# Own rows of layer 1: nine places in place of six

## The chip, the cores and the metric

The kernel runs on one core of one Trainium2 chip. The metric is the device time of one execution in microseconds. Four runs of the kernel before gave 989.70, 991.78, 993.73 and 992.79 us, with a median of 992.29 us.

## The reference, cut to what matters

The program is a stack of four graph layers over 2708 nodes with 512 features each. `adj` is a sparse matrix with a full diagonal, about five values in a row. Every layer ends in a residual sum and a layernorm. Layer 1, which the change is about, is this:

```python
type_sum_a = adj_a @ x
type_sum_b = adj_b @ x
attn_a = sigmoid(concatenate([type_sum_a, x], axis=1) @ Wa.T + ba)
attn_b = sigmoid(concatenate([type_sum_b, x], axis=1) @ Wb.T + bb)
h = x @ W_sa
s_left = h @ a_sa[0, :Hd]
s_right = h @ a_sa[0, Hd:]
scores = s_left[:, None] + s_right[None, :]
e = where(adj_a != 0, exp(-leaky_relu(scores, 0.01)), 0.0)
attn = e / (sum(e, axis=1, keepdims=True) + 1e-05)
x_a = attn @ h
x_b = adj_b @ (x @ W_gcnb) + b_gcnb
x = layernorm(x + sigmoid(attn_a * x_a + attn_b * x_b))
```

`adj_a` and `adj_b` are both `adj`. Layer 0 before it gives `layernorm(x + (x - (adj @ x) * (d + 1)) @ W + b)`. Layers 2 and 3 are sums over neighbours again, layer 3 with a last matmul and a tanh.

## The kernel before, in words

All is float32. The 2708 nodes are cut into 24 blocks of 113 rows (`R`, the last has 109), and for the dense products of layer 0 into 22 windows of 128 rows. Layer 0 finds the values of each block of `adj` off the diagonal and lists them in four chunks (`EC`) of 128 edges. From then on a sum over neighbours is, for each block, four indirect gathers of source rows (`gather`, L600, issued on the POOL queue) and matmuls of the gathered rows with a spread matrix of the edges' values. The diagonal is left out of the lists, so each block also needs its *own rows*, scaled by the diagonal.

For every window layer 0 computes `h` and `x @ W_gcnb` and stores both, with five more columns, as one row of 1029 floats (`W1`) in the DRAM table `table[0]` (`store0`, L1051). Layer 1 gathers whole rows from this table (`gather1`, L1371) into a ring of three buffers `gath`, and the own rows of block `i` are loaded from it by `load_own1(i)` (L634): 112 rows and 1 row of 1024 floats, two DMAs on the SP queue (`move_rows`, L564). They land in one of six places (`own_place`, L630): two in each of `shared[0]`, `shared[1]` and `w0_sb`, buffers that layer 0 uses for blocks of `adj` and for its weight.

The order is written out by hand: the instructions stand on every engine and queue as the program lists them. The places around the change are these:

- the end of layer 0 (loop at L1209 to L1283): blocks 0 to 3 are loaded in the step `k + 2 == NB` (L1263), blocks 4 and 5 in the step `k == NB` (L1280). After the loop come `keep_busy(4)`, eight matmul instructions that nobody reads, and the store of the last window, `store0(KB - 1)` (L1285);
- between the layers: `bg_bc` is loaded (L1499), small tables are made on DVE (L1308 to L1330), and `spread_left` (L1363) turns a column of `xr` into rows with PE transposes and DVE copies;
- layer 1's loop: step `i` issues `gather1(i + 2)`, then `sums1(i)` (PE, L1407), `both1(i - 1)` (DVE, with `l1a` at L1458), then `load_own1(i - 1 + NO)` into the place that `both1(i - 1)` has just read, then `scored_sums1(i)` (PE, L1417), `scores1(i + 1)` (DVE, `e` at L1390, the first that needs all of block `i + 1`'s gathers), `stats1(i - 1)`, `gates1(i)`, `gated1(i)` (DVE, `l1b` at L1437, the first reader of own rows), `mask1(i + 1)`, and `norm1(i - 1)`, which stores block `i - 1` of layer 1's result with two DMAs on the SP queue.

With `NO = 6` the loop loads blocks 6 to 23 in its steps 1 to 18; steps 19 to 23 load none.

Layer 0 also has these small rings from the pool `work`: two tiles `xi` (a block's own rows of `x`), two tiles `uT` (turned rows, also used by layer 3) and three tiles `uw` (turned windows).

Of the kernel before, what the change touches and what calls it, by code (L numbers as in the profile page):

```python
# [8 lines left out]
FP = mybir.dt.float32  # L9
# [3 lines left out]
P = 128  # L13
# [434 lines left out]
def sparse_stack(  # L448
# [30 lines left out]
    N, D = x.shape  # L479
# [4 lines left out]
    DB = D // P  # L484

    W1 = 2 * D + 5
# [4 lines left out]
    big = ctx.enter_context(tc.tile_pool(name="big", bufs=1))  # L491
    work = ctx.enter_context(tc.tile_pool(name="work", bufs=2))
    small = ctx.enter_context(tc.tile_pool(name="small", bufs=4))

    def rows(i):
        return min(R, N - i * R)
# [41 lines left out]
    def column(name, value):  # L538
        t = const.tile([P, NB], FP, name=name)
        nc.gpsimd.memset(t, value)  # L540
        return t
# [4 lines left out]
    adiag = column("adiag", 1.0)  # L546
# [17 lines left out]
    def move_rows(r, dst, src):  # L564

        c = r // 16 * 16
        for a, b in ((0, c), (c, r)):
            if a < b:
                nc.sync.dma_start(out=dst(a, b), in_=src(a, b))

    def turned(u, r, name):

        tr = ps_tr.tile([P, DB, P], FP, tag="tr", name=f"tr_{name}")
        for f in range(DB):
            nc.tensor.transpose(tr[:, f, :r], u[:r, f * P : (f + 1) * P], ident[:r, :r])
        uT = work.tile([P, DB, P], FP, tag="uT", name=f"uT_{name}")
        nc.scalar.copy(uT[:, :, :r], tr[:, :, :r])  # L577
        return uT

# [44 lines left out]

    shared = [big.tile([P, KB * R], FP, name=f"shared{k}") for k in range(2)]

    w0_sb = big.tile([P, DB, D], FP, name="w0_sb")
    NO = 6

    def own_place(i):  # L630
        t = (*shared, w0_sb.rearrange("p b d -> p (b d)"))[i % NO // 2]
        return t[:, i % 2 * 2 * D :][:, : 2 * D]

    def load_own1(i):  # L634
        r = rows(i)
        own1[i] = own_place(i)
        move_rows(
            r, lambda a, b: own1[i][a:b, :],
            lambda a, b: table[0][i * R + a : i * R + b, 1 : 2 * D + 1],
        )  # L640

    own1 = {}
# [5 lines left out]
    with ExitStack() as phase:  # L648
# [40 lines left out]

        def load_own(i):  # L690
            r = rows(i)
            xi = work.tile([P, D], FP, tag="xi", name=f"xi{i}")
            move_rows(r, lambda a, b: xi[a:b, :], lambda a, b: x[i * R + a : i * R + b, :])
            return xi

# [13 lines left out]
        def wrows(w):  # L709
            return min(P, N - w * P)  # L710
# [92 lines left out]
        w_saT = {}  # L803
# [14 lines left out]
        def turn_w(k):  # L818
            ps = ps_tr.tile([P, DB, P], FP, tag="tr", name=f"w_sa_t{k}")
            for f in range(DB):  # L820
                nc.tensor.transpose(ps[:, f, :], w_sa_sb[:, f, k * P : (k + 1) * P], ident)
            wT = work.tile([P, DB, P], FP, tag="uT", name=f"w_saT{k}")
            nc.scalar.copy(wT, ps)
            w_saT[k] = wT

# [74 lines left out]
        def ranges(i):  # L900

            t = made[i]
            nc.vector.scalar_tensor_tensor(
                rec_all[:, i, 2, :], t["ahead"].to_broadcast([P, NS]), -0.5, t["far"],
                op0=ALU.mult, op1=ALU.add,
            )

        def mark(i):
            q = made[i]["q"]
            nc.vector.tensor_scalar(q, q, made[i]["total"], None, op0=ALU.is_lt)  # L910
# [140 lines left out]
        def store0(w):  # L1051
            r = wrows(w)
            st, o = st0.pop(w)
            nc.scalar.copy(st[:r, D + 1 : 2 * D + 1], o[:r, :])
            move_rows(
                r, lambda a, b: table[0][w * P + a : w * P + b, :], lambda a, b: st[a:b, :]
            )

        window_uT = {}

        def turn_u(i):

            u, r = u0.pop(i), rows(i)
            tr = ps_tr.tile([P, DB, P], FP, tag="tr", name=f"tr_l0_{i}")
            for f in range(DB):
                nc.tensor.transpose(tr[:, f, :r], u[:r, f * P : (f + 1) * P], ident[:r, :r])
            a = i * R
            while a < i * R + r:
                w = a // P
                b = min(i * R + r, (w + 1) * P)  # L1070
                if w not in window_uT:
                    window_uT[w] = work.tile(
                        [P, DB, P], FP, tag="uw", name=f"uw{w}", bufs=3
                    )
                nc.scalar.copy(
                    window_uT[w][:, :, a - w * P : b - w * P], tr[:, :, a - i * R : b - i * R]
                )
                a = b

        def turn_x(w):  # L1080
            turned0["x", w] = turned(x1w[w % 2], wrows(w), f"x1_{w}")
# [127 lines left out]
        for k in range(NB + 2):  # L1209
            m = k + 2  # L1210
            w, wx, rest = window_at.get(k), window_at.get(k - 1), window_at.get(k - 1)
            bare = 2 < k < NB and w is None
            after = 2 < k < NB and wx is None
            parts = 4
            if any(t not in window_at for t in (k + 1, k + 2, k + 3)) and 2 < k < NB - 4:
                parts = 5
            if bare:
                parts, rest = 2, None
            if after:
                parts, rest = 3, window_at[k - 2]  # L1220
            if wx is not None and k <= NB:
                turn_x(wx)
            if m < NB:
                ranges(m)
                mark(m)
                fetch(m)
            if w is not None:
                project0(w)
            if k == 1:
                times_a(2)  # L1230
                times_a(3)
            if k == 0:
                times_a(0)
                turn_w(2)
            if unstored:
                store0(unstored.pop())
            if k + 3 < NB:
                negatives(k + 3)
            search(1)
            if m < NB:  # L1240
                pick(m)
                own[m] = load_own(m)
                values0(m)
            if k == 1:
                score_rows()
            if w is not None:
                bias0(w)
            search(1)
            if w is not None:
                residual0(w)  # L1250
            if window_at.get(k + 1, 0) > 1:
                load_window(window_at[k + 1])
            search(parts - 2)
            if wx is not None and not bare:
                next0(wx)
            if w is not None:
                norm0(w)
            if k + 1 < NB:
                sums0(k + 1)
                inputs0(k + 1)  # L1260
            if k == 1:
                score_columns()
            if k + 2 == NB:  # L1263
                worst = check_lists()
                for i in range(4):
                    load_own1(i)
            if k == 0:
                times_a(1)
                turn_w(3)
            if bare:  # L1270
                starts(m + 1)
                next0(wx)
            elif rest is not None:
                rest0(rest, lambda: turn_x(w) if k == NB else starts(m + 1) if m + 1 < NB else None)
                unstored.append(rest)
            elif m + 1 < NB:
                starts(m + 1)
            if k + 1 < NB:
                turn_u(k + 1)
            if k == NB:  # L1280
                tell(worst)
                for i in range(4, NO):
                    load_own1(i)  # L1283
        keep_busy(4)
        store0(KB - 1)  # L1285


    gpool = ctx.enter_context(tc.tile_pool(name="gpool", bufs=1))
# [61 lines left out]
    def halves(t, r):  # L1350
        return t[:r, :].rearrange("p (k d) -> p k d", k=2)
# [81 lines left out]
    def gated1(i):  # L1433

        r = rows(i)
        vb = vb1[i] = spool.tile([P, D], FP, tag="vb", name=f"l1b{i}")
        nc.vector.scalar_tensor_tensor(  # L1437
            halves(vb, r), halves(own1[i][:, D:], r), adiag[:r, i : i + 1],
            sum_s.pop(i)[:r, :, :H], op0=ALU.mult, op1=ALU.add,
        )  # L1440
        nc.vector.tensor_add(vb[:r, :], vb[:r, :], bg_bc[:r, :])
        gate = gate1[i]
        nc.vector.tensor_scalar(
            gate[:r, :], gate[:r, :], 0.5, 0.5, op0=ALU.mult, op1=ALU.add
        )
        nc.scalar.activation(vb[:r, :], vb[:r, :], AF.Copy, scale=gate[:r, 1:2])
# [148 lines left out]
    for i in range(NB):  # L1595
# [3 lines left out]
        if i > 0:  # L1599
            both1(i - 1)  # L1600
        if 0 < i and i - 1 + NO < NB:
            load_own1(i - 1 + NO)
        if i + 2 < NB:
# [197 lines left out]
    for i in range(NB + 1):  # L1801
        if i + 2 < NB:
            gather(gath[(i + 2) % NGB], i + 2, table[2], D)
        if i > 0:
            uT = turned(u3.pop(i - 1), rows(i - 1), f"l3_{i - 1}")
# [67 lines left out]
```

## Time and profile before

| | |
|---|---|
| median of four runs | 992.29 us |
| profiled execution, its own time | 989.72 us |
| its span | 987.6 us |
| PE busy | 888.2 us (90%) |
| DVE busy | 686.0 us (69%) |
| DMA issues of own rows, in the loop of layer 1 | 435.5 to 579.6 us from the span's start |
| gathers of layer 1, first and last issue | 414.2 and 606.4 us |

The span is what lies between the first and the last recorded instruction; the time of the execution is 2.1 us longer. The four runs spread over 4.03 us, and the profiled execution is as fast as the fastest of them. PE's 90% is an average over the whole program: in layer 0 it is busy without a gap, in layer 1 it isn't. The busy share of the DMA engines, slice by slice, tells the stages apart better.

### The profile page before, as it was taken

To read this page: it belongs to the slowest core of one execution; us is meant where nothing else is said; L and a number is where in the kernel's file an instruction comes from. 1 tells how busy PE (TensorE), PEld (TensorE's weight loads), DVE (VectorE), ACT (ScalarE), POOL (GpSimd) and SP (SyncE) were. 2 spreads that over 40 slices of the span, in tenths; PEclk is the share of its full clock that TensorE was granted. 3 is DMA by queue.
4 is the path that set the end of the run, shared out by engine and by line. 5 is a ranking of instruction groups with operands and counts; after the bars stand their busy time and mean duration, and the time that the engine had idled before them with its cause. 6 is when DMAs were issued, how large, how long until landed. Compare 5 with 4: busy or idle time off the path is not lost.

```text
span 987.6 us, 11188 instructions
## 1 busy us (share of the span) xinstructions
PE 888.2 (90%) x2957; PEld 495.6 (50%) x2957; DVE 686.0 (69%) x1807; ACT 527.1 (53%) x1221; POOL 469.6 (48%) x536
## 2 busy tenths in 40 slices
PE   6789999999999999998888989796797879999994
PEld 2445556555655555466666767422232334444441
DVE  7787899878998832268888889756586525655543
ACT  5676767766768743457776766334354412222222
POOL 3323233413223310166666665476676476776640
PEclk7779999999999999989999999997999998999998
DMA  9977786978886534489999995366676454555531
GB/s 245 311 196 202 219 233 191 270 221 228 220 226 201 174 119 135 124 295 296 302 303 316 297 319 185 104 197 182 201 214 186 145 169 135 171 162 163 168 106 35
DMA packets 133516, 201.70 MB, mean 204 GB/s; under 512 B 82456, under 2 KB 82502, under 8 KB 133445
## 3 DMA queue, kind: packets, MB, share of 16 engines
q0 software_dynamic: 36864, 111.73, 37.8%
q1 hardware_dynamic: 96581, 89.18, 31.5%
q8 instruction: 26, 0.43, 0.2%
q14 instruction: 45, 0.37, 0.1%
HBM read 181.83 MB, written 27.80 MB: 212 GB/s over the span
## 4 chain that ended last, share of the span: by engine, by line
PE 60%; DVE 14%; DMA 9%; issue 6%; ACT 3%; POOL 3%; another core or an unknown queue 2%; SPq 2%; POOLq 0%; DVEq 0%; ACTq 0%
PE o_l L584 15%; PE l3a L613 8%; PE l2a L613 8%; PE hb L584 7%; PE h L584 7%; PE l0a L613 6%; DMA gath<-table,source 6%; PE unread L1537 2%; POOL gath L600 2%; PE fetched L915 2%; SPq L677 2%; DMA gath<-in_x_dram 1%; DVE st_l L1476 1%; DVE l1b L1437 1%
## 5 line engine op out<-in xcount | busy, mean ns | idle before, releaser
L600 POOL DMA_INDIRECT gath<-table,source x288 | 316.6, 1099 | 167.5 <-issue 79.3
L600 POOL DMA_INDIRECT gath<-in_x_dram,source x96 | 98.0, 1020 | 224.5 <-issue 192.3
L1407 PE MATMUL l1s<-gath,s 128*113 128x256 f32 (+3 forms) x384 | 94.9, 402 | 23.0 <-DVE l1b L1437 22.5
L613 PE MATMUL l2a<-gath,s_left 128*113 128x512 f32 (+1 forms) x192 | 92.5, 619 | 4.8 <-DMA gath<-table,source 3.7
L1407 PEld LDWEIGHTS l1s<-gath,s 128*113 128x113 f32 (+1 forms) x384 | 69.7, 186 | 48.4 <-DVE l1b L1437 29.9
L613 PE MATMUL l3a<-gath,s 128*113 128x512 f32 (+1 forms) x192 | 90.0, 612 | 3.0 <-DMA gath<-table,source 3.0
L613 PE MATMUL l0a<-gath,s 128*113 128x512 f32 (+1 forms) x192 | 87.4, 598 | 0.0
L584 PE MATMUL o_l<-shared,uT_l 128*113 128x512 f32 (+1 forms) x192 | 86.5, 593 | 0.7 <-ACT uT_l L577 0.7
L1417 PE MATMUL l1e<-gath,e 128*113 128x257 f32 (+3 forms) x384 | 87.0, 379 | 0.0
L584 PE MATMUL hb<-w_gc_sb,uT_x 128*128 128x512 f32 (+1 forms) x176 | 83.3, 601 | 0.0
L584 PE MATMUL o_l<-w_sb,uw 128*128 128x512 f32 (+1 forms) x176 | 82.9, 615 | 0.2
L584 PE MATMUL h<-w_sa_sb,uT_x 128*128 128x259 f32 (+1 forms) x352 | 80.8, 382 | 0.0
L1417 PEld LDWEIGHTS l1e<-gath,e 128*113 128x113 f32 (+1 forms) x384 | 68.0, 177 | 15.3 <-issue 0.2
L584 PEld LDWEIGHTS h<-w_sa_sb,uT_x 128*128 128x128 f32 (+1 forms) x352 | 64.8, 185 | 19.8 <-issue 6.1
L1792 ACT ACTIVATE y<-l3v,mv_l 113x512 f32<-113x512 f32 (+1 forms) x24 | 19.5, 813 | 82.5 <-DVE mv_l L1788 74.8
L1537 PE MATMUL unread<-bg_bc,ident 128*128 128x512 f32 x80 | 41.1, 627 | 24.4 <-remote 18.2
L613 PEld LDWEIGHTS l2a<-gath,s_left 128*113 128x113 f32 (+1 forms) x192 | 32.8, 185 | 54.9 <-issue 35.8
L1766 DVE SCALAR_TENSOR_TENSOR l3v<-o_l,d_inv,b_bc 113x512 f32<-113x512 f32 (+1 forms) x25 | 18.1, 729 | 58.3 <-PE o_l L584 54.9
L584 PEld LDWEIGHTS o_l<-shared,uT_l 128*113 128x113 f32 (+1 forms) x192 | 33.9, 178 | 48.9 <-issue 48.0
L613 PEld LDWEIGHTS l3a<-gath,s 128*113 128x113 f32 (+1 forms) x192 | 33.2, 184 | 42.6 <-issue 38.7
L613 PEld LDWEIGHTS l0a<-gath,s 128*113 128x113 f32 (+1 forms) x192 | 34.1, 180 | 39.9 <-issue 35.8
L1294 DVE TENSOR_SCALAR s<-niota_r,nrow,edges 128x113 f32<-128x113 f32 x192 | 51.3, 341 | 0.0
(244 smaller groups left out, 1585.8 us busy)
## 6 DMA issues: line engine op xcount, KB each, us to landing
shared<-in_adj_dram SPq DMA_DIRECT2D x14, 1186.5 KB
table<-st SPq DMA_DIRECT2D x21, 514.5 KB
gath<-in_adj_dram SPq DMA_DIRECT2D x7, 1186.5 KB
shared<-table SPq DMA_DIRECT2D x16, 448.0 KB
gath<-in_x_dram SPq DMA_DIRECT2D x21, 256.0 KB
xi<-in_x_dram SPq DMA_DIRECT2D x23, 224.0 KB
table<-xr SPq DMA_DIRECT2D x23, 224.0 KB
table<-y SPq DMA_DIRECT2D x23, 224.0 KB
```

The costliest lines, as they stand in the source:

```text
L584: nc.tensor.matmul(o, lhsT=uT[:, f, :r], rhs=w[:, f, :], start=(f == 0), stop=(f == DB - 1))
L600: nc.gpsimd.indirect_dma_start(out=g[:, c, :n], out_offset=None, in_=src[:, :], in_offset=bass.IndirectOffsetOnAxis(ap=source[:, i, c : c ...
L613: nc.tensor.matmul(agg[:r, :], lhsT=s[:, c, :r], rhs=g[:, c, off : off + D], start=(c == 0), stop=(c == EC - 1),)
L677: nc.sync.dma_start(out=a[:TAIL, NF, :r], in_=adjT[NF * P :, at])
L915: nc.tensor.matmul(t["fetched"][:, c, : 3 * NS], lhsT=t["q"][:, c * P : (c + 1) * P], rhs=rec_all[:, i].rearrange("p k s -> p (k s)"), sta ...
L1294: nc.vector.tensor_scalar(s[:, c, :], niota_r, nrow[:, i, c : c + 1], edges[:, i, c, 1:2], op0=ALU.is_equal, op1=ALU.mult,)
L1407: nc.tensor.matmul(sum_s[i][:r, k, : at.stop - at.start], lhsT=s[:, c, :r], rhs=g[:, c, at], start=(c == 0), stop=(c == EC - 1),)
L1417: nc.tensor.matmul(sum_e[i][:r, k, k : k + at.stop - at.start], lhsT=e[:, c, :r], rhs=g[:, c, at], start=(c == 0), stop=(c == EC - 1),)
L1437: nc.vector.scalar_tensor_tensor(halves(vb, r), halves(own1[i][:, D:], r), adiag[:r, i : i + 1], sum_s.pop(i)[:r, :, :H], op0=ALU.mult, op ...
L1537: nc.tensor.matmul(o[:, :cols], lhsT=ident, rhs=bg_bc[:, :cols], start=True, stop=True)
L1766: nc.vector.scalar_tensor_tensor(v[:r, at], o[:r, at], d_inv[:r, i : i + 1], b3_bc[:r, at], op0=ALU.mult, op1=ALU.add,)
L1792: nc.scalar.activation(y[:r, :], v[:r, :], AF.Identity, bias=mv[:r, 3:4], scale=mv[:r, 2:3])
```

## The change

Layer 1 has nine places for own rows in place of six. Three new places lie in memory that layer 0 uses for other things: the tiles `uw` become parts of one buffer `uw_own` (one place), and the tiles `xi` and `uT` become parts of one buffer `xi_own` (two places, the first over both `xi`, the second over both `uT`). The rings keep their lengths and their turn. A place is now 1029 floats long, and 1024 of them are used, so every second place starts 4116 bytes behind the first of its buffer (4096 before).

The own rows of block 6 are loaded with those of blocks 4 and 5; those of blocks 7 and 8 behind the store of layer 0's last window. In the loop, step `i` loads block `i + 8` in place of block `i + 5`, so steps 1 to 15 load blocks 9 to 23, and steps 16 to 18 load none any more.

```diff
+    def next_uT():
+        uT_ring.append(uT_ring.pop(0))
+        return uT_ring[-1]
+
     def turned(u, r, name):
...
-        uT = work.tile([P, DB, P], FP, tag="uT", name=f"uT_{name}")
+        uT = next_uT()
         nc.scalar.copy(uT[:, :, :r], tr[:, :, :r])
...
-    w0_sb = big.tile([P, DB, D], FP, name="w0_sb")
-    NO = 6
+    w0_own = big.tile([P, 2 * W1], FP, name="w0_sb")
+    w0_sb = w0_own[:, : DB * D].rearrange("p (b d) -> p b d", d=D)
+
+    uw_own = big.tile([P, 3 * D], FP, name="uw_own")
+    uw_ring = [uw_own[:, k * D : (k + 1) * D].rearrange("p (b i) -> p b i", i=P) for k in range(3)]
+    xi_own = big.tile([P, max(4 * D, 2 * W1)], FP, name="xi_own")
+    xi_ring = [xi_own[:, k * D : (k + 1) * D] for k in range(2)]
+    uT_ring = [
+        xi_own[:, k * D : (k + 1) * D].rearrange("p (b i) -> p b i", i=P) for k in range(2, 4)
+    ]
+    NO = 9
 
     def own_place(i):
-        t = (*shared, w0_sb.rearrange("p b d -> p (b d)"))[i % NO // 2]
-        return t[:, i % 2 * 2 * D :][:, : 2 * D]
+        k = i % NO
+        t = (*shared, w0_own, uw_own, xi_own)[(k + (k >= 7)) // 2]
+        return t[:, (k + (k >= 7)) % 2 * W1 :][:, :W1]
 
     def load_own1(i):
         r = rows(i)
         own1[i] = own_place(i)
         move_rows(
-            r, lambda a, b: own1[i][a:b, :],
+            r, lambda a, b: own1[i][a:b, : 2 * D],
             lambda a, b: table[0][i * R + a : i * R + b, 1 : 2 * D + 1],
         )
...
-            xi = work.tile([P, D], FP, tag="xi", name=f"xi{i}")
+            xi = xi_ring[i % 2]
...
-                    window_uT[w] = work.tile(
-                        [P, DB, P], FP, tag="uw", name=f"uw{w}", bufs=3
-                    )
+                    window_uT[w] = uw_ring[w % 3]
...
             if k == NB:
                 tell(worst)
-                for i in range(4, NO):
+                for i in range(4, 7):
                     load_own1(i)
         keep_busy(4)
         store0(KB - 1)
+        for i in range(7, NO):
+            load_own1(i)
...
-            halves(vb, r), halves(own1[i][:, D:], r), adiag[:r, i : i + 1],
+            halves(vb, r), halves(own1[i][:, D : 2 * D], r), adiag[:r, i : i + 1],
```

`turn_w` takes its `wT` from `next_uT()` too.

More of the change, by code (lines that the diff above doesn't have):

```diff
@@ L821, in turn_w @@
                 nc.tensor.transpose(ps[:, f, :], w_sa_sb[:, f, k * P : (k + 1) * P], ident)
-            wT = work.tile([P, DB, P], FP, tag="uT", name=f"w_saT{k}")
+            wT = next_uT()
             nc.scalar.copy(wT, ps)
```

## The prediction

> **What bounds the kernel now.** I first read the stretches of 60 us, for the stages (busy time of PE, PEld, DVE, ACT and POOL, then granted clock, DMA share, GB/s):
>
> ```profile
> 360.00:420.00 60.00, 58.24 (x200) 29.99 (x198) 17.48 (x51) 22.52 (x65) 4.55 (x5) 0.98 0.42 125
> 480.00:540.00 60.00, 51.15 (x229) 39.77 (x228) 50.18 (x129) 42.45 (x106) 41.05 (x43) 1.00 0.98 308
> 600.00:660.00 60.00, 50.99 (x170) 29.07 (x169) 47.11 (x138) 25.57 (x58) 32.08 (x34) 0.97 0.49 150
> ```
>
> Layer 1 (414 to 632 us) is where the DMA engines are full: share 0.98 at 308 GB/s, while PE and DVE both have idle time. The end of layer 0 is the contrary: PE is never idle, and DMA is used at 0.42.
>
> Second, the DVE instruction that first needs a block's whole gathers (`e`, L1390), in order of time, with the idle time before it. These are blocks 17 to 23, and ahead of them block 2:
>
> ```profile
> 436.29 0.62 DVE L1390 TENSOR_TENSOR e<-gath,s_left 128x452 f32<-128x452 f32 x1
> ...
> 563.76 0.63 DVE L1390 TENSOR_TENSOR e<-gath,s_left 128x452 f32<-128x452 f32 x1 [0.42 <-DMA gath<-table,source]
> 572.54 0.63 DVE L1390 TENSOR_TENSOR e<-gath,s_left 128x452 f32<-128x452 f32 x1 [1.08 <-DMA gath<-table,source]
> 580.60 0.63 DVE L1390 TENSOR_TENSOR e<-gath,s_left 128x452 f32<-128x452 f32 x1 [0.35 <-issue]
> 589.88 0.63 DVE L1390 TENSOR_TENSOR e<-gath,s_left 128x452 f32<-128x452 f32 x1 [1.58 <-issue]
> 597.51 0.62 DVE L1390 TENSOR_TENSOR e<-gath,s_left 128x452 f32<-128x452 f32 x1
> 605.12 0.62 DVE L1390 TENSOR_TENSOR e<-gath,s_left 128x452 f32<-128x452 f32 x1
> 612.70 0.62 DVE L1390 TENSOR_TENSOR e<-gath,s_left 128x452 f32<-128x452 f32 x1
> ```
>
> The three last distances are 7.63, 7.61 and 7.58 us, with no wait in front of `e`: here the engines set the pace, and the gathers keep up. Before that a step takes (589.88 - 436.29) / 18 = 8.53 us and DVE waits for gathers. What differs is the SP queue (issues of own rows and of the stores of results):
>
> ```profile
> 562.64 0.69 SPq L569 DMA_DIRECT2D shared<-table  x2
> 570.04 0.63 SPq L569 DMA_DIRECT2D table<-xr  x2
> 570.76 0.63 SPq L569 DMA_DIRECT2D w_sb<-table  x2
> 578.83 0.63 SPq L569 DMA_DIRECT2D table<-xr  x2
> 579.55 0.79 SPq L569 DMA_DIRECT2D w_sb<-table  x2
> 586.89 32.72 SPq L569 DMA_DIRECT2D table<-xr  x10
> ```
>
> The loads of own rows end at 579.55. Block 20's gathers, issued beside that last load, are the last that DVE waits for. So in layer 1 the DMA engines bound the steps that load own rows, by about 0.9 us each, and nothing bounds the later ones but PE and DVE.
>
> Third, the seam between the layers: what SP and POOL issue there, then stretches of 2 us.
>
> ```profile
> 402.78 1.47 SPq L569 DMA_DIRECT2D w_sb<-table  x4
> 404.34 0.35 SPq L569 DMA_DIRECT2D table<-st  x1
> 407.48 1.28 SPq L569 DMA_DIRECT2D xr<-gath  x2
> 411.07 0.69 SPq L569 DMA_DIRECT2D table<-st  x2
> 413.34 0.23 SPq L1499 DMA_DIRECT2D bg_bc<-in_L_gnn_b_gcnb_dram  x1
> ```
>
> ```profile
> 414.23 1.00 POOL L600 DMA_INDIRECT gath<-table,source  x1 [55.55 <-PE unread L799]
> ```
>
> ```profile
> 406.00:408.00 2.00, 2.00 (x8) 0.66 (x7) 0.00 (x0) 0.47 (x3) 0.00 (x0) 1.00 0.99 337
> 412.00:414.00 2.00, 2.00 (x5) 0.57 (x3) 1.28 (x7) 0.57 (x2) 0.00 (x0) 1.00 0.13 25
> 414.00:416.00 2.00, 1.26 (x9) 1.02 (x8) 1.97 (x9) 1.42 (x5) 1.47 (x2) 1.00 0.07 13
> 416.00:418.00 2.00, 1.49 (x9) 1.10 (x10) 1.70 (x4) 1.93 (x7) 1.52 (x2) 0.82 0.86 282
> ```
>
> The last store of layer 0 (411.07) has landed by 413.34, when SP's wait for it ends; the first gather is issued at 414.23, and its data move from about 415.8. Between 410 and 415.8 the DMA engines are nearly idle.
>
> **The change part by part.** *Loads taken out of the loop.* Steps 16, 17 and 18 lose a pair of DMAs each (448 and 4 KB, 0.463 MB; issues at 562.64, 570.76 and 579.55). Steps 1 to 15 load as before, only for a later block. The last pair is then that of 553.56, which lies beside block 17's gathers; `e` of block 17 stays as it is, and the three distances behind it, 589.88 - 563.76 = 26.12 us, become three of 7.61 us, 22.83 us: 3.29 us less. Do the gathers keep up by then? In the distances without own rows they did, three times. With the mean step of 8.53 us instead of these three I would get 3 x 0.92 = 2.8 us. I take 3.29, since the places are named, and keep 2.8 as the other end. More than 3.3 is excluded as long as 7.61 us is the floor: of it PE works 3.74 us (sums) and 3.62 us (scored sums). What is late next is that pair; the seven distances to layer 1's end, and layer 2 behind it, start earlier by as much.
>
> *Block 6, loaded behind blocks 4 and 5.* Its two issues (1.47 / 4 = 0.37 us each) go ahead of the store at 404.34 on the SP queue, which moves to about 405.1. Behind that store SP waits anyway until 407.48. The 0.463 MB at 337 GB/s are 1.37 us, so the DMA engines are done at about 410 in place of 408.6, and the small moves into `xr` of 407.48 land 1.4 us later. The first DVE instruction between the layers waits for them (L1308, 410.08); its three instructions end at 410.71, and ACT, which comes next, is busy until 412.36 with the store's copy and a table load. 412.1 is before 412.36, so I take 0, with 0 to 1 us as the bounds.
>
> *Blocks 7 and 8, loaded behind the last store.* Four issues, 1.47 us, from 411.78 to 413.25, ahead of `bg_bc`, which waits for that store until 413.34 anyway; its row then lands behind 0.926 MB, at about 417.5, and is first read at 421.45 (PE, L1511). Their memory is free (the last PE reader ends at 410.4). The pairs issued at 402.78 moved from about 404.3, 1.5 us later; so these move from 413.3, for 0.926 MB / 337 GB/s = 2.75 us, to 416.05. Against the gathers' start at 415.8 this is 0.25 us of overlap. I take 0.25; the bounds are 0 (the gap holds all) and 2.75 us (all of it ahead of the gathers, whose data then run without a gap to `e` of block 1).
>
> *Places that start 4116 bytes on.* Same bytes and packets as before. The nearest row is the gather itself: its rows go into chunks of 4128 bytes, from source rows 4116 bytes apart, at 308 GB/s in the stretch above, beside 337 for the aligned places. I take 0. The Trainium skill ("DMA: Bandwidth & Descriptors", section "How a descriptor splits into AXI transactions") says that a descriptor which doesn't start on a 256-byte boundary costs an extra, partly wasted transaction; by it a 4096-byte row costs at most 7 beats more on 128, an estimate of 5%, or some 0.08 us on each of the odd places' loads, 0.6 us in all, and the sum would be -2.4 us in place of -3.0. The source rows began off such a boundary before the change too, and no row here shows the price.
>
> *The rings* keep their lengths and turn, and layer 0's instructions stand in the same order and wait for the same work: 0. No engine instruction is added or removed.
>
> **Sum:** -3.29 + 0.25 = -3.04 us. The profiled execution's 989.72 us (987.6 of span and 2.1 around) becomes 986.7. It was the fastest of the runs; the median of four, 992.29, lies 2.6 us above it, and I carry that along: **989.2 us**, 0.31% less. About 0.3% (3 us) is what a measurement of this kernel can tell from no change, so the forecast stands on that edge.
>
> **The rivals.**
> 1. *The seam eats the gain.* The loads of blocks 7 and 8 go between the first gathers, and everything behind is late by up to 2.75 us. For it: those gathers' data move without a gap from 416 to 428, so a delay isn't made good. Against it: an idle gap of nearly the right length. Time: 992.29 - 3.29 + 1.5 (the middle) = 990.5; within 0.3%.
> 2. *The loop doesn't get faster:* the gathers of blocks 18 to 20 are late for another reason, such as POOL's issues (four of about 1.3 us behind a wait), and the change does nothing to see. Against it: the three distances without loads. Time: 992.3.
> 3. *The seam gets slower than the loop gains.* The last store is reported only when the reads behind it on the queue are through. All of layer 1 waits for that report: the gathers, and DVE's tables at L1324 with the PE transposes behind them. It is then 2.75 us late, and PE, which the profile shows at a granted clock of 0.50 from 418, stays there longer: block 0's sums took 5.75 us against 3.74 at full clock; 2.0 us more of this gives 992.29 - 3.29 + 2.75 + 2.0 = 993.8. It decides once the seam costs more than 3.29 us. With all 16 matmuls at the 0.77 us of the half clock it would be 6.5 in place of 2.0, and 998. Against it: the store's data are ahead in the queue and were landed 2.3 us after issue.
> 4. *Odd places slow down their loads.* About half of 15 loads lie in bound steps, 1.5 us each at 308 GB/s; it takes 30% on each to eat 3.3 us, and 55% for 3 us of loss (995.3). Nothing in the profile speaks for it.
>
> **How the numbers follow.** The forecast has a chance of 0.47, with a range of its own of 988.2 to 990.4; rival 1 has 0.25, rival 2 0.07, rival 3 0.15 (a third of it within 0.3%), rival 4 0.06. So faster 0.47, within 0.3% 0.25 + 0.07 + 0.05 = 0.37, slower 0.10 + 0.06 = 0.16. The range goes from 992.29 - 3.3, with half the spread of the four runs (2.0) off, 987.0, to rival 3's 993.8 with a little for the spread, 994.5.
>
> **What would show it.** Right: SP issues no own rows after about 554; `e` of blocks 18 to 20 comes without a wait, at distances near 7.6 us; the DMA share between 413 and 416 is near 1; the first gather is issued at about 414.2, and `e` of block 1 lies as far behind it as before (15.6 us). Wrong: `e` of block 1 late by over 1 us, a first gather late by over 1 us, waits for gathers that stay in blocks 18 to 20, or longer steps in the first fifteen.

## The result, and the profile after

The changed kernel is faster: a median of 986.31 us over 42 runs, against 991.17 us for the kernel before over 63 runs, the four given above among them. The ratio is 0.9946, with a 95% interval of 0.9932 to 0.9960, that is 0.40 to 0.68% less. It is a ratio of means without the changed kernel's five slow runs (over 1.5% above its fastest; the kernel before has none), so it flatters the change a little. Over all runs the means differ by 4.5 us, or 0.45%, with a standard error of 0.7 us; the standard error says how far chance alone typically moves such a difference. I had forecast 0.31% less and 989.2 us, with a range down to 987.0. The direction was right, the time lies 0.7 us below the range, and the gain of this comparison, 4.9 us by the medians, is 1.6 times the sum of 3.04 us.

The execution that was profiled with this comparison took 991.91 us, 5.6 us above the median of its kernel. The lines here are therefore from another execution of the same kernel (e4 below): 984.68 us, with a span of 982.5.

The stretches of 60 us (columns as before):

```profile
360.00:420.00 60.00, 57.68 (x197) 30.16 (x196) 18.06 (x52) 23.56 (x67) 5.85 (x6) 0.96 0.52 154
480.00:540.00 60.00, 50.99 (x228) 39.60 (x227) 50.73 (x128) 43.39 (x110) 41.64 (x45) 1.00 0.98 309
600.00:660.00 60.00, 49.67 (x152) 25.39 (x150) 43.60 (x127) 23.96 (x52) 31.61 (x33) 0.97 0.48 146
```

The middle of layer 1 is as it was (0.98 at 308 GB/s before). The end of layer 0 moves more: a DMA share of 0.52 in place of 0.42.

The DVE instruction that first needs a block's whole gathers, blocks 16 to 23:

```profile
552.78 0.63 DVE L1404 TENSOR_TENSOR e<-gath,s_left 128x452 f32<-128x452 f32 x1 [0.49 <-DMA gath<-table,source]
561.15 0.63 DVE L1404 TENSOR_TENSOR e<-gath,s_left 128x452 f32<-128x452 f32 x1 [0.63 <-DMA gath<-table,source]
568.77 0.62 DVE L1404 TENSOR_TENSOR e<-gath,s_left 128x452 f32<-128x452 f32 x1
576.39 0.62 DVE L1404 TENSOR_TENSOR e<-gath,s_left 128x452 f32<-128x452 f32 x1
584.00 0.62 DVE L1404 TENSOR_TENSOR e<-gath,s_left 128x452 f32<-128x452 f32 x1
591.83 0.63 DVE L1404 TENSOR_TENSOR e<-gath,s_left 128x452 f32<-128x452 f32 x1
599.66 0.63 DVE L1404 TENSOR_TENSOR e<-gath,s_left 128x452 f32<-128x452 f32 x1
607.25 0.62 DVE L1404 TENSOR_TENSOR e<-gath,s_left 128x452 f32<-128x452 f32 x1
```

Block 17 still waits for a gather; blocks 18 to 20 don't. Their distances are 7.62, 7.62 and 7.61 us, 22.85 in all, where the kernel before had 26.12. That is the forecast's 22.83.

The seam, as SP and POOL issue it:

```profile
401.02 1.46 SPq L569 DMA_DIRECT2D w_sb<-table  x4
402.53 0.63 SPq L569 DMA_DIRECT2D uw_own<-table  x2
403.26 0.35 SPq L569 DMA_DIRECT2D table<-st  x1
405.73 1.27 SPq L569 DMA_DIRECT2D xr<-gath  x2
409.32 0.69 SPq L569 DMA_DIRECT2D table<-st  x2
410.10 1.36 SPq L569 DMA_DIRECT2D xi_own<-table  x4
411.74 0.24 SPq L1513 DMA_DIRECT2D bg_bc<-in_L_gnn_b_gcnb_dram  x1
...
551.60 0.97 SPq L569 DMA_DIRECT2D w_sb<-table  x2
559.10 55.06 SPq L569 DMA_DIRECT2D table<-xr  x16
```

```profile
412.62 1.00 POOL L604 DMA_INDIRECT gath<-table,source  x1 [55.69 <-PE unread L813]
```

```profile
410.00:412.00 2.00, 2.00 (x6) 0.76 (x4) 0.98 (x6) 0.82 (x2) 0.00 (x0) 1.00 0.73 146
412.00:414.00 2.00, 1.51 (x9) 1.02 (x8) 1.91 (x6) 0.54 (x2) 1.07 (x2) 1.00 0.96 299
414.00:416.00 2.00, 0.34 (x2) 0.34 (x3) 1.99 (x8) 1.93 (x6) 1.70 (x2) 0.82 0.95 289
```

The loads of block 6 (402.53) and of blocks 7 and 8 (410.10) stand where the program puts them, and the last own rows are issued at 551.60. The last store is issued 1.75 us earlier here than in the trace of before, so the stretches have to be counted from it: in the 5 us from its issue on the DMA share was 0.14 at 24 GB/s, and is 0.75 at 202 GB/s now. Most of the idle gap is filled; the stretch from 414 on belongs to the gathers already. The first gather comes 3.30 us behind the issue of the last store (409.32); before it was 3.16. `e` of block 1 comes 18.64 us behind it; before it was 18.77. So in this trace the seam costs nothing that shows at `e` of block 1.

### The profile page after: what moved, and what is told of

It reads as the page before. It is cut to its first block, busy times and chain, and to the rows that moved or that the text cites. A ratio compares the mean times of both kernels' runs of the same rounds, so it can differ in the third digit from the quotient of the medians.

```text
span 989.8 us, 11189 instructions
## 1 busy us (share of the span) xinstructions
PE 892.2 (90%) x2957; PEld 493.5 (50%) x2957; DVE 685.6 (69%) x1807; ACT 527.0 (53%) x1221; POOL 467.3 (47%) x536
## 4 chain that ended last, share of the span: by engine, by line
PE 63%; DMA 12%; DVE 8%; issue 5%; POOL 4%; another core or an unknown queue 3%; ACT 3%; SPq 2%; POOLq 0%; DVEq 0%; ACTq 0%
PE o_l L588 15%; DMA gath<-table,source 9%; PE l3a L617 8%; PE l2a L617 8%; PE hb L588 7%; PE h L588 7%; PE l0a L617 6%; PE unread L1551 3%; POOL gath L604 3%; PE fetched L929 2%; PE l1s L1421 2%; SPq L691 1%; DMA gath<-in_x_dram 1%; PE tr_l L579 1%
## 5 line engine op out<-in xcount | busy, mean ns | idle before, releaser
L617 PE MATMUL l2a<-gath,s_left 128*113 128x512 f32 (+1 forms) x192 | 97.3, 647 | 4.7 <-DMA gath<-table,source 4.2
L588 PE MATMUL o_l<-shared,xi_own 128*113 128x512 f32 (+1 forms) x192 | 86.5, 593 | 1.5 <-issue 0.8
L588 PE MATMUL hb<-w_gc_sb,xi_own 128*128 128x512 f32 (+1 forms) x176 | 83.3, 601 | 0.0
L588 PE MATMUL o_l<-w_sb,uw_own 128*128 128x512 f32 (+1 forms) x176 | 82.2, 611 | 0.2
L588 PE MATMUL h<-w_sa_sb,xi_own 128*128 128x259 f32 (+1 forms) x352 | 80.8, 382 | 0.0
L588 PEld LDWEIGHTS h<-w_sa_sb,xi_own 128*128 128x128 f32 (+1 forms) x352 | 64.8, 185 | 19.8 <-issue 6.1
L588 PEld LDWEIGHTS o_l<-shared,xi_own 128*113 128x113 f32 (+1 forms) x192 | 33.9, 178 | 49.8 <-issue 49.0
```

Source lines behind the costliest of these rows:

```text
L588: nc.tensor.matmul(o, lhsT=uT[:, f, :r], rhs=w[:, f, :], start=(f == 0), stop=(f == DB - 1))
L617: nc.tensor.matmul(agg[:r, :], lhsT=s[:, c, :r], rhs=g[:, c, off : off + D], start=(c == 0), stop=(c == EC - 1),)
```

## The experiments

The theory: all of the gain lies in the distances of blocks 18 to 20, because three loads left a stage that the DMA engines bound, and their new places cost next to nothing. The rival: since the first comparison shows 4.9 us, something else gains too, in the buffers or at the seam. To tell them apart I use the times and one stretch of each trace: from the issue of layer 0's last store to `e` of block 23.

| run | kernel | store to `e` of block 23 | of it, blocks 17 to 20 | ratio to before, 95% interval |
|---|---|---|---|---|
| | before | 201.63 | 26.12 | |
| | changed, first comparison | 198.51 | 22.85 | 0.9946 (0.9932 to 0.9960) |
| e6 | before | 200.85 | 26.00 | 0.9994 (0.9973 to 1.0015) |
| e1 | new buffers, six places | 200.84 | 26.23 | 0.9993 (0.9963 to 1.0023) |
| e3 | changed, three loads put back | 201.86 | 26.51 | 1.0006 (0.9984 to 1.0027) |
| e2 | before, last three loads left out | 197.83 | 23.15 | 0.9987 (0.9957 to 1.0017) |
| e4 | changed | 197.93 | 22.85 | 0.9981 (0.9953 to 1.0010) |
| e5 | changed | 196.24 | 22.97 | 0.9971 (0.9946 to 0.9996) |
| e9 | changed | 198.31 | 22.84 | 0.9981 (0.9955 to 1.0008) |
| e10 | changed | 198.32 | 22.85 | 0.9984 (0.9955 to 1.0013) |
| e7 | ten places | 199.26 | 22.85 | 0.9954 (0.9934 to 0.9973) |
| e11 | ten places | 198.35 | 23.16 | 0.9954 (0.9927 to 0.9981) |
| e8 | no loads in the loop | 184.88 | 22.93 | 0.9845 (0.9820 to 0.9871) |

Runs e1 to e4 shared one chip, e5 to e8 a second one, e9 to e11 a third. The second is faster throughout (970.47 us for the kernel before, 987.78 and 987.83 on the others), so only ratios and differences are compared across them.

**e1, the layout alone.** The changed kernel, but with six places and the loads where they were:

```diff
-    NO = 9
+    NO = 6
...
-                for i in range(4, 7):
+                for i in range(4, NO):
                     load_own1(i)
...
-        for i in range(7, NO):
-            load_own1(i)
```

> The new buffers, rings and places of 1029 floats, but six places and the loads of own rows in the steps where they were before the change. My theory (the gain is the three loads that left steps 16 to 18, and nothing else): no change, within 1 us of the kernel before. Rival (the change gained 4.9 us by the medians where steps 16 to 18 account for 3.1, so the rest comes from the buffers, for instance from rings without a pool's waits): 1.5 to 2 us faster. If places 4116 bytes apart cost something, it is slower, by up to 0.6 us.

No change that shows: 987.94 us against 987.78, and a stretch of 200.84, as in the kernel before. By the times alone the rival's 1.5 to 2 us are not excluded (the means are 0.6 us faster, with a standard error of 1.3); in the stretch the rings and the places of 4116 bytes neither gain nor cost. The bound steps, from `e` of block 2 to that of block 17, took 126.64 us, against 127.47 in the trace of before, though half of their loads went to odd places.

**e2, the last three loads left out.** The kernel before:

```diff
-        if 0 < i and i - 1 + NO < NB:
+        if 0 < i and i - 1 + NO < NB - 3:
             load_own1(i - 1 + NO)
+        elif 0 < i and i - 1 + NO < NB:
+            own1[i - 1 + NO] = own_place(i - 1 + NO)
```

> The kernel before, with the loads of own rows in steps 16 to 18 left out and nothing loaded in their place: blocks 21 to 23 of layer 1 take the own rows of blocks 15 to 17, so their output is not the reference's. My theory: the three distances of e in blocks 18 to 20 become 7.6 us, 3.3 us less in all, and the whole kernel is 2.8 to 3.3 us faster. If the seam costs something, this kernel is faster than the changed one by as much (0.25 us by my sum, up to 2.75). Rival (part of the changed kernel's gain is made in the seam): this kernel is 1.5 to 2 us slower than the changed one.

In the trace it does what the changed kernel does, without the loads at the seam: 197.83 us to `e` of block 23, with blocks 18 to 20 at 7.62, 7.62 and 7.91 us apart. The time moved by 1.4 us by the medians, in an interval of -0.43 to +0.17%, which holds the 2.8 to 3.3 us expected and also zero. The changed kernel beside it stands at 0.9981, so neither a cost nor a gain of the seam is seen, within the 0.3% that such an interval leaves open.

**e3, the three loads put back.** The changed kernel, with loads of the same size in steps 16 to 18 into places that are free by then:

```diff
         if 0 < i and i - 1 + NO < NB:
             load_own1(i - 1 + NO)
+        elif 0 < i and i + 5 < NB:
+            move_rows(
+                rows(i + 5), lambda a, b: own_place(i - 1)[a:b, : 2 * D],
+                lambda a, b: table[0][(i + 5) * R + a : (i + 5) * R + b, 1 : 2 * D + 1],
+            )
```

> The changed kernel, blocks 6 to 8 loaded early, but steps 16 to 18 issue loads of own rows again, of the same size and in the same order on the queue, into places that are free by then, where nobody reads them. My theory: the distances of e in blocks 18 to 20 are 26 us again, and the kernel stands 0 to 0.3 us behind the kernel before. Rival (the seam gains): still 1.5 to 2 us faster than before.

The gain is gone. Its trace shows the three issues again, and behind them the waits of blocks 18 to 20:

```profile
562.27 0.65 SPq L569 DMA_DIRECT2D uw_own<-table  x2
569.46 0.63 SPq L569 DMA_DIRECT2D table<-xr  x2
570.21 0.68 SPq L569 DMA_DIRECT2D xi_own<-table  x2
579.03 0.89 SPq L569 DMA_DIRECT2D table<-xr  x2
580.03 0.79 SPq L569 DMA_DIRECT2D xi_own<-table  x2
```

```profile
572.75 0.63 DVE L1404 TENSOR_TENSOR e<-gath,s_left 128x452 f32<-128x452 f32 x1 [1.87 <-DMA gath<-table,source]
581.51 0.63 DVE L1404 TENSOR_TENSOR e<-gath,s_left 128x452 f32<-128x452 f32 x1 [1.05 <-DMA gath<-table,source]
589.68 0.63 DVE L1404 TENSOR_TENSOR e<-gath,s_left 128x452 f32<-128x452 f32 x1 [0.46 <-DMA gath<-table,source]
```

Early loads at the seam with late ones kept: 1.0006, no faster than before. So the gain comes from what left the loop, and the three early loads go into time in which the DMA engines were largely idle. `e` of block 1 came 18.27 us behind the last store.

**e4, e5, e9 and e10, the changed kernel again**, and **e6, the kernel before against itself.**

> The changed kernel once more, beside the other three on the same chip. My theory: 3 to 3.5 us faster than before; by the runs so far 4.9 us by the medians and 4.5 by the means. In its trace the stretch from the issue of layer 0's last store to e of block 23 is 198 to 199 us (201.6 before), and what lies behind block 23 is as long as before, but for differences between single executions.

> The changed kernel, beside the kernel before submitted as a kernel of its own, to see whether the 4.9 us by the medians of the first comparison are more than the trace accounts for. My theory (all of the gain lies in the distances of blocks 18 to 20): about 3.2 us faster than before, with the stretch from layer 0's last store to e of block 23 at 198 us; the other 1.7 us are spread between executions. Rival (something outside layer 1's loop gains too): 4.5 to 5 us again, and one of the other stretches is shorter by 1 to 2 us.

> The changed kernel again. My theory: 3.2 to 3.7 us faster than before (0.33 to 0.38%), and the stretch from layer 0's last store to e of block 23 lasts 196 to 199 us, of which the distances of blocks 18 to 20 take 22.9. Rival (a further gain outside those distances): 4.9 us.

> As the run before, for a second set of times on the same chip: the same 3.2 to 3.7 us by my theory, 4.9 by the rival.

> The kernel before, unchanged, timed against itself. Both theories: a ratio of 1 within its interval; how far it stands from 1 is what such a comparison can be off by. In its trace the stretch from the last store to e of block 23 is 201 to 202 us.

The stretch does what was expected: in five traces of the changed kernel (four here, and the first with 198.51) it has a mean of 197.86 us, in the four kernels that keep the loads (before twice, e1, e3) 201.30. That is 3.4 us (standard error 0.5), of which 3.3 lie in blocks 18 to 20 (22.87 against 26.22), the part that scatters least. The 4.9 us did not come back: the medians moved by 1.5 to 2.6 us. The means of the 48 runs on three chips, weighted by their spread, are 2.4 us below those of the kernel before, with a standard error of 0.6. The same sum over the runs of the first comparison gives 4.5 us with 0.7. The traces' 3.4 us lie between the two, within two standard errors of either, and the two sums together give 3.2 us with a standard error of 0.4. So a further gain isn't shown, and e6 says how far such a comparison moves by itself: 0.5 us by the means.

**e8, no loads in the loop.** The kernel before:

```diff
         if 0 < i and i - 1 + NO < NB:
-            load_own1(i - 1 + NO)
+            own1[i - 1 + NO] = own_place(i - 1 + NO)
```

> The kernel before without any load of own rows in the loop of layer 1: blocks 6 to 23 take the rows that blocks 0 to 5 left, so their output is not the reference's. My theory (the transfers bound all steps that load): the 18 distances of e from block 2 to block 20 fall from 8.53 to 7.6 us, 16.6 us in all. Rival (only the last three loads mattered, the earlier waits for gathers come from their own bytes or from POOL's issue): 3 to 6 us.

The strongest of the runs: 956.22 us (five runs) against 970.47, a ratio of 0.9845. The stretch fell from 200.85 us (e6, same chip) to 184.88, by 16.0 us. Of this, 15.35 us lie in the 18 distances from block 2 to block 20 (153.07 us in e6, 137.72 here), where 16.6 were expected: 0.85 us for each load. The 18 distances were 7.61 to 7.96 us. Here are blocks 7 to 10 in the trace of before, then the same blocks in e8, and the stretch of 60 us of e8 that begins with block 8:

```profile
479.50 0.63 DVE L1390 TENSOR_TENSOR e<-gath,s_left 128x452 f32<-128x452 f32 x1 [1.59 <-DMA gath<-table,source]
487.12 0.62 DVE L1390 TENSOR_TENSOR e<-gath,s_left 128x452 f32<-128x452 f32 x1
496.00 0.65 DVE L1390 TENSOR_TENSOR e<-gath,s_left 128x452 f32<-128x452 f32 x1 [1.19 <-DMA gath<-table,source]
504.28 0.63 DVE L1390 TENSOR_TENSOR e<-gath,s_left 128x452 f32<-128x452 f32 x1 [0.55 <-DMA gath<-table,source]
```

```profile
473.89 0.62 DVE L1390 TENSOR_TENSOR e<-gath,s_left 128x452 f32<-128x452 f32 x1
481.50 0.62 DVE L1390 TENSOR_TENSOR e<-gath,s_left 128x452 f32<-128x452 f32 x1
489.12 0.62 DVE L1390 TENSOR_TENSOR e<-gath,s_left 128x452 f32<-128x452 f32 x1
496.73 0.62 DVE L1390 TENSOR_TENSOR e<-gath,s_left 128x452 f32<-128x452 f32 x1
```

```profile
480.00:540.00 60.00, 56.26 (x252) 43.61 (x251) 54.70 (x139) 46.46 (x119) 47.64 (x48) 1.00 0.86 282
```

With 0.86 of the DMA engines in use the gathers keep up in all 18 steps but one (0.25 us before block 11), and PE rises from 51.15 to 56.26 us of 60. A load came back with less than its transfer: 0.463 MB at 308 GB/s are 1.5 us, and 0.85 us were saved, because below 7.6 us the step is bound by the engines. Whether the bytes or the number of DMAs set the price isn't separated here, as every load has the same size. POOL's issue doesn't bound the steps (it was a condition of my second rival): it issues as many gathers, in less time.

**e7 and e11, ten places.** If a load out of a bound step is worth 0.9 us, a tenth place should bring as much again. The records of the edges have three planes of which two are read by nobody after layer 0; laid side by side they hold one more place. The loads of blocks 7 and 9 move to those of blocks 0 to 3:

```diff
-    rec_all = const.tile([P, NB, 3, NS], FP, name="rec_all")
+    rec_all = const.tile([P, 3, NB, NS], FP, name="rec_all")
+    rec_flat = rec_all.rearrange("p k b s -> p (k b s)")
...
-    NO = 9
+    NO = 10
...
         k = i % NO
+        if k == 9:
+            return rec_flat[:, : 2 * D]
...
-                for i in range(4):
+                for i in (0, 1, 2, 3, 7, 9):
                     load_own1(i)
...
-                for i in range(4, 7):
+                for i in (4, 5, 6):
                     load_own1(i)
...
-        for i in range(7, NO):
-            load_own1(i)
+        load_own1(8)
```

(The planes are now far, code, value; the places that read or write them follow.)

> Ten places: the changed kernel, with a tenth in the edge records' two planes that nobody reads after layer 0 (their order is turned so that these two lie side by side), and the loads of blocks 7 and 9 issued with those of blocks 0 to 3, in a part of layer 0 in which DMA has time; only block 8 is left at the seam, and step 15 loads nothing either. My theory: each load out of a bound step is worth what a step with own rows costs over one without, 0.9 to 1.1 us, so about 1 us less than the changed kernel, 4.2 us less than before: e of block 17 comes without a wait too, and the stretch to e of block 23 is 197 us. Rival (the seam's transfers are hidden and more of them cost nothing, but the loads in layer 0 get in the way of its stores): no better than the changed kernel, with layer 0's last store later.

> The kernel with ten places again, beside the changed kernel on the same chip. My theory: 0.9 to 1.1 us faster than the changed kernel, 4.1 to 4.8 us faster than before, with four distances of e (blocks 17 to 20) at 7.6 us. Rival: no better than the changed kernel.

By the medians it is the fastest kernel that computes everything: 966.37 us beside 968.79 for the changed one, and 982.40 beside 985.28 and 986.31. By the means it is 1.0 us (standard error 1.1) and 2.4 us (1.0) ahead of the changed kernel, of which the first can't be told from nothing. Block 17 comes without a wait, as expected (here blocks 16 to 18 of e7):

```profile
552.08 0.63 DVE L1407 TENSOR_TENSOR e<-gath,s_left 128x452 f32<-128x452 f32 x1 [1.67 <-DMA gath<-table,source]
559.69 0.62 DVE L1407 TENSOR_TENSOR e<-gath,s_left 128x452 f32<-128x452 f32 x1
567.31 0.62 DVE L1407 TENSOR_TENSOR e<-gath,s_left 128x452 f32<-128x452 f32 x1
```

But the stretch was not 197 us: 199.26 and 198.35. The steps ahead of block 16, which are bound by transfers in this kernel too, took 120.2 and 119.7 us from block 2 on, against 117.2 to 118.5 in the traces of the changed kernel. That is 1.9 us more, about twice the 1.0 us that the free step gave, so the stretch is 0.9 us longer than the changed kernel's mean of 197.86: the price of a load, as e8 gives it, did not come back for the tenth place. What is ahead of it is shorter instead: the last store of layer 0 was issued at 406.82 us on the second chip (408.58 in e5, 408.23 in e6, but 411.43 in e8, whose layer 0 is that of the kernel before) and at 408.75 on the third (411.86 and 409.96). Whether the new order of the planes or the earlier loads do that, or chance in two executions, I did not test. That it beats the kernel before is measured; that the tenth place is what does it is not shown.

## Why the prediction was right or wrong

*Loads taken out of the loop (3.29 us): right, in place and size.* The three distances became 22.84 to 22.97 us in five traces, 22.83 forecast. The other end, 2.8, goes by the mean price, which was 0.85 us for each load in e8, 2.6 us for three. One reading was freer than its view: the idle times ahead of `e` of blocks 19 and 20 (0.35 and 1.58 us) stand there as "issue", time without a visible cause, and I took them for waits for gathers. The changed kernel bears this out: without the loads they are gone. The floor of 7.61 us held for 18 steps in e8, but for single ones of up to 7.96.

*Block 6 (0): right in the number, wrong in its reason.* I took 0 because ACT would still be busy when DVE's tables came. They came later than that. DVE's first instruction between the layers came 1.3 us behind the issue of the last store (0.9 to 1.6 us in the five traces), in place of 1.0 us ahead of it, so it started 2.3 us later (1.9 to 2.5) where I had 1.4. ACT waited for it, 0.26 to 0.94 us in the five traces; in e4:

```profile
410.63 0.20 DVE L1322 TENSOR_TENSOR ediag<-xr 128x24 f32<-128x24 f32 x1 [8.72 <-DMA xr<-gath]
```

```profile
411.29 0.22 ACT L1319 ACTIVATE ediag<-ediag 128x24 f32<-128x24 f32 x1 [0.69 <-DVE ediag L1318]
```

The delay went on to PE, whose second group of transposes (`spread_left`) began 5.55 to 6.35 us behind the last store's issue (5.44 before), and was made good behind them: block 0's sums began 9.65 to 11.83 us behind it, and 9.97 to 12.35 in the five traces with the old seam (before, e1, e2, e6 and e8). That there was such slack I had not worked out; the 0 was luck to that extent.

*Blocks 7 and 8 (0.25): in agreement, but too small to be shown.* From the last store to `e` of block 1 the changed kernel took 18.00 to 18.85 us in five traces, the five with the old seam 17.91 to 18.77. The means are 18.62 and 18.36, 0.26 us apart with a standard error of 0.23: the forecast's 0.25 fits, and so does nothing at all. Rivals 1 and 3 (the seam eats the gain, or more) fall with that and with e3. In rival 3 the first gather should have been late; it came 3.25 to 3.33 us behind the issue of the last store in the five traces of the changed kernel, 3.16 to 3.18 with the old seam: 0.1 us.

*Odd places (0): right.* e1 shows no loss in the bound steps. The extra 0.6 us that I had estimated from the Trainium skill ("DMA: Bandwidth & Descriptors", "How a descriptor splits into AXI transactions") is not seen, though 0.6 us is less than these 127 us differ between executions (125.1 to 127.5). (My working had at most 7 beats more on 128; with a start off a multiple of 32 bytes, as 4116 is, it is at most 8, and the estimate 0.7 us.) Rival 4, which needs a loss of over 3 us, falls.

*Rival 2 (nothing to see)* falls with the distances themselves, and e8 shows that it was the transfers.

*What failed is the level that the sum started from, and the allowance around it.* The sum of -3.04 us describes the traces (-3.4 us, with 3.3 in the three distances). But the forecast of 989.2 started from 992.29 us, the median of four runs, and its lower end, 987.0, allowed half the spread of those four (2.0 us) below it. Over 63 runs the kernel before lies between 984.02 and 998.17 us, and its median is 991.17: the starting level was 1.1 us too high. Four runs can't fix it better, since medians of four drawn from these 63 lie between 987.4 and 993.9 in 95 of 100 draws. From 991.17 the sum alone gives 988.1, and the range by its own working would have gone down to 985.9, with the measured 986.31 inside.

The other 1.8 us between 988.1 and 986.31 I can't place. No stretch that the change touches has them, and by the medians the four repeats gave less than the sum (1.5 to 2.6 us), not more. By the means, the first comparison and the four repeats together give 3.2 us with a standard error of 0.4, which fits the sum. What made the first comparison larger stays open: chance, or the scatter of layers 2 and 3 (below), are what I would look at first.

## What to carry to other kernels

In a stage that the transfers bound, a transfer that can be moved elsewhere has a price, and in a stage with idle DMA engines it can cost next to nothing (0.1 us at the first gather here). The price is not the transfer's own time (1.5 us here) but what the step has above the pace of its engines (0.85 us in the mean), and it need not come back for one more load, as ten places show. Find it by looking for steps of the same loop that don't have the transfer (here the last ones), and the room by looking for memory that the stage before has finished with. A change of 0.3% is better verified by a stretch of the trace that contains it than by the total, which here ran from 984 to 998 us for one and the same kernel.

## What the runs showed of the hardware

The part of the program that has nothing to do with the change scatters most. From `e` of block 23 to the end, the same code took 374.5 to 376.9 us in the trace of before and in six of the seven on the first and third chips (e1 to e4, e10, e11), but 368.6 us in e9, 380.9 us in the first profile of the changed kernel, and 356.7 to 358.8 us in the four on the second chip. Most of this lies in layers 2 and 3, from the first store of layer 2's results on: 318.9 to 322.0 us on the second chip, 330.5 to 343.4 elsewhere. In that part PE's granted clock dips (0.89 to 0.91 in stretches of 60 us of the first profile of the changed kernel), and where the dips fall differs from execution to execution. From that store on, the mean granted clock was 0.98 to 0.99 in the four executions on the second chip, and 0.94 to 0.96 in all others; the shortest of the others (e9, 330.5 us) had 0.96, the longest (343.4 us) 0.94. So the length of this part goes with its clock. That the clock causes it isn't shown, and I did not test what sets it.
